# A cap of four on the half-chunk transfers under way in the passes of a Fourier-layer kernel

## The chip, the cores and the metric

The kernel runs on one core of a Trainium2 chip. The metric is the device time of one execution in microseconds (us). Before the change it is 11834.71 us, the median of three runs (11832.55 to 11845.82). All profiles are of one profiled execution.

## The reference, cut to what matters

64 images of 256 x 256 go through four Fourier layers with 32 channels; the result, with 77 text rows appended, goes through one transformer layer. Only the Fourier layers matter here:

```python
v = concat([x, gx, gy]) @ p_w + p_b                  # (64, 32, 256, 256)
for i in range(4):
    x1 = irfft2(mixed low modes of rfft2(v))          # 24 x 12 modes kept
    x2 = einsum('bcxy,cd->bdxy', v, w_w[i]) + w_b[i]
    v  = batchnorm(x1 + x2)                           # mean and variance over b, x, y
    if i < 3: v = relu(v)
out = einsum('bcxy,cu->bxyu', v, q_w) + q_b
...
h = concat([out, txt], axis=1)                        # then attention and a feed-forward with top-k
```

The tensor `v` of one image is 32 x 256 x 256 float32, 8 MB, so that all 64 images do not fit on the chip: `v` goes to device memory after each layer and comes back for the next. The normalisation needs sums over all images, so one layer ends before the next begins.

## The kernel before, in words

The program runs in this order: a first transform of the input and the mixing of modes (to about 200 us of the span); then three **passes**, `layer(0)`, `layer(1)` and `layer(2)`, with mixing of modes between them (`mix`, lines 389 to 486); and a last stage from about 9125 us, which reads `v` once more and runs the transformer (lines 810 to 1147). Pass 0 runs from about 200 to 2749 us, pass 1 from 2884 to 5904, pass 2 from 6041 to 9052.

**A pass** (`layer`, line 531) goes over 64 images of 8 chunks each. A chunk is a tile of 128 partitions x 8 x 256 float32, 1 MB. For a chunk `(b, t)` the function `chunk` (line 732) does this:

- `pre` (line 619): TensorE builds the spectral part from `y_` (line 624: 16 matmul instructions) and, in passes 1 and 2, adds the channel mix of the chunk `vin` loaded from memory (line 635: 32 instructions). ScalarE then writes the first half of the new chunk `vo` through a relu (line 642) and SyncE's queue issues the store of that half, 512 KB (line 643). VectorE writes the second half (line 647; ScalarE at t = 6, line 645) and its store follows (line 648).
- `load_v` (line 585), in passes 1 and 2: the chunk that is needed four chunks later is loaded in two halves of 512 KB (line 589).
- `product` (line 660): the channel mix of the new chunk (line 667: 32 matmul instructions) whose squares ScalarE sums (line 674).
- `turn` (line 650): VectorE transposes the chunk for the coming transform (line 655).

Once per image, at t = 3, TensorE also runs the whole forward transform of the image before (`along_y`, line 685, 256 matmul instructions, and `along_x`, line 712), three products and the `spread` of the next half (line 606). In that stretch few chunks are finished, and few stores issued.

**The order of the work** is written out by hand (the pass is built under `manual_schedule`): each engine runs its instructions in the order of the code. All the transfers of a pass stand in one queue, SyncE's (SP's), in the order store, store, load, load for each chunk; at t = 3 two small loads `ams` (line 573, for the image after the next) and one small store `xh` (line 720) follow. SP is in order: while its head waits, all later transfers wait too.

**What limits the transfers under way before the change.** The completion of SP's transfers is told by eight semaphores, taken in turn. A transfer waits until the one before it on its semaphore has landed, so it waits for the transfer issued eight earlier: at most eight of SP's transfers are under way. Besides, a store needs its half of `vo` written; a load needs a free `vin` buffer (four of them, line 551: the buffer is free when `pre` of four chunks earlier has read it); and a `vo` buffer (four of them, line 553) is written again only when its stores have landed.

In pass 0 there are no chunk loads. Pass 0 loads four small pieces of the image per image instead (`mv`, line 580).

Of the kernel before, what the change touches and what calls it, by code (L numbers as in the profile page):

```python
# [135 lines left out]
def tile_fno_fusion_transformer(ctx: ExitStack, tc: tile.TileContext, a, cst_d, grid_d, out):  # L136
    nc = tc.nc
# [370 lines left out]
    def layer(i, st, src, dst, acc):  # L508
# [7 lines left out]
        with ExitStack() as cx:  # L516
# [47 lines left out]
            y_, t32, vin, vo = {}, {}, {}, {}  # L564

            def two_banks():

                ring[0] += 1
                return pp.tile([128, 2, 512], F32, name=f"ring{ring[0] % 4}")

            def load_am(b):
                for n in range(2):
                    nc.sync.dma_start(
                        ams[b % 2][64 * n:64 * n + 2 * KX],
                        mix_d[i][b].rearrange("p k c -> (p k) c")[:, 512 * n:512 * n + 512],
                    )
# [8 lines left out]
            def load_v(b, t):  # L585
                vin[b, t] = ip.tile([128, 8, S], F32, name="vin")
                for n in range(2):
                    rows = slice(4 * n, 4 * n + 4)
                    nc.sync.dma_start(vin[b, t][:, rows], src[b][:, t, rows])

            def scale_am(b):
                for _, p0, cs in halves:
# [21 lines left out]
            def four():  # L614

                t2 = [two_banks() for _ in range(2)]
                return t2, [t2[n // 2][:, n % 2] for n in range(4)]

            def pre(b, t):
                t2, ps = four()  # L620
                for r in range(2):
                    for n in range(4):
                        q = 8 * (t % 4) + 4 * r
                        nc.tensor.matmul(  # L624
                            ps[n][:, 256 * r:256 * r + 256],
                            lhsT=y_[b, t // 4][32 * n:32 * n + K, q:q + 4, :].rearrange("p q c -> p (q c)"),
                            rhs=mv[b % 2][32 * n:32 * n + K, 2 * t + r, :] if i == 0 else T4[32 * n:32 * n + K, :],
                            start=r == 0, stop=i == 0, skip_group_check=True,
                        )
                if i:  # L630
                    v = vin.pop((b, t))
                    for k in range(4):
                        for n in range(4):
                            j = (n + k) % 4
                            nc.tensor.matmul(  # L635
                                ps[n][32 * j:32 * j + 32], lhsT=ws[32 * n:32 * n + 32],
                                rhs=v[32 * n:32 * n + 32, 2 * j:2 * j + 2, :], start=False, stop=True,
                                skip_group_check=True, tile_position=(32 * n, 32 * j),
                            )
                o = vo[b, t] = op.tile([128, 8, S], F32, name="vo")  # L640
                of = o.rearrange("p (n r) y -> p n (r y)", r=2)
                nc.scalar.activation(of[:, 0:2], t2[0], AF.Relu)  # L642
                nc.sync.dma_start(dst[b][:, t, 0:4], o[:, 0:4])
                if t == 6 or i == 0 and t == 1:
                    nc.scalar.activation(of[:, 2:4], t2[1], AF.Relu)  # L645
                else:
                    nc.vector.tensor_scalar(of[:, 2:4], t2[1], 0.0, None, ALU.max)  # L647
                nc.sync.dma_start(dst[b][:, t, 4:8], o[:, 4:8])

            def turn(b, t):  # L650

# [52 lines left out]
            def along_x(b):  # L704
# [15 lines left out]
                nc.sync.dma_start(xh_d[i][:, b, :], xo.rearrange("p g k -> p (g k)"))  # L720

            load_am(0)
            load_am(1)
            if i == 0:
                load_x(0)
            else:
                for t in range(4):
                    load_v(0, t)
# [3 lines left out]
            def chunk(b, t, done=None):  # L732
                pre(b, t)
                nb, nt = (b, t + 4) if t < 4 else (b + 1, t - 4)
                if i and nb < B:
                    load_v(nb, nt)
                if done is not None:
                    product(*done)
                if t == 5 and b + 1 < B:
                    spread(b + 1, 0)  # L740
                turn(b, t)

            for b in range(B):
                for t in range(8):
                    if b and t == 3:


                        t2, _ = four()
                        along_y(b - 1, t2, range(0, 3))
                        product(b, 0)  # L750
                        along_y(b - 1, t2, range(3, 5))
                        ring[0] -= 2
                        chunk(b, 3)
                        along_y(b - 1, t2, range(5, 8))
                        ring[0] -= 2
                        product(b, 1)
                        product(b, 2)
                    else:
                        last = (b, t - 1) if t else (b - 1, 7)
                        chunk(b, t, None if last[0] < 0 or b and t in (1, 2) else last)  # L760
                    if t == 3:
                        spread(b, 1)
                        if b + 2 < B:
                            load_am(b + 2)
                        if b:
                            along_x(b - 1)
                    if i == 0 and t == 0 and b + 1 < B:
                        load_x(b + 1)
                    if t == 7 and b + 2 < B:
                        scale_am(b + 2)  # L770
# [6 lines left out]
    for i in range(L):  # L777
# [26 lines left out]
        if i < L - 1:  # L804
            acc = const.tile([128, 16 * B], F32, name="acc") if acc is None else acc
            with tc.manual_schedule():
                layer(i, st, vd[(i + 1) % 2], vd[i % 2], acc)


    src = vd[L % 2]  # L810
# [87 lines left out]
    rows = [128, 128, TXT]  # L898
# [283 lines left out]
```

## Time and profile before

| what | value |
|---|---|
| median of 3 runs | 11834.71 us |
| the profiled execution's own time | 11830.89 us |
| its span, first to last instruction | 11829.1 us |
| mean granted TensorE clock | 0.976 |
| TensorE (PE) busy | 10902.5 us, 92% |
| VectorE (DVE) busy | 8539.0 us, 72% |
| ScalarE (ACT) busy | 6507.0 us, 55% |
| HBM read and written | 1761.87 MB and 1696.92 MB |
| stores `v<-vo` | 3072 of 512 KB |
| loads `vin<-v` | 2048 of 512 KB |

The page gives the busy time of each engine, then the span cut into 40 equal slices (295.7 us each) with the busy share of each engine in tenths, the busy share of the 16 DMA engines and the rate in GB/s. Passes 1 and 2 are slices 10 to 31 or so. A wait is shown with what released it; "issue" means that the engine waited for nothing that the profile can name. The queue q1 carries SP's transfers, q8 carries the engines' instruction blocks. Beside the page the trace holds each packet of each DMA queue (start, duration, bytes) and each increment of the semaphores that tell of a landing; a transfer of 512 KB is 128 packets of 4096 bytes, eight on each of the 16 DMA engines, and its landing is 16 increments, one from each DMA engine.

### The profile page before, as it was taken

Reading aid. Unit: us, or ns where it says so; the run is one execution under the profiler, and the core shown is the slowest. Engines: PE = TensorE matmul, PEld = TensorE weight load, DVE = VectorE, ACT = ScalarE, POOL = GpSimd, SP = SyncE. Lnnn points to the kernel's source line nnn. Section 1 sums busy time; section 2 is a strip of 40 time slices with the busy share of each in tenths; the row PEclk is TensorE's granted clock in tenths of the full one; section 3 lists DMA queues with packets and bytes.
Section 4 is the critical chain, followed back from the end, with each engine's and each line's share of the span. In section 5 each row is a group of like instructions: output and inputs, shape, how many; then the busy total and the mean of one; then the engine's idle time right before and its main releaser. Section 6 shows DMA issues by size and latency. Waiting matters only on the chain. (4 is left out here: it accounts for less than half of the span.)

```text
span 11829.1 us, 409923 instructions
## 1 busy us (share of the span) xinstructions
PE 10902.5 (92%) x182038; PEld 5901.9 (50%) x182038; DVE 8539.0 (72%) x10405; ACT 6507.0 (55%) x10697; POOL 1327.2 (11%) x1987
## 2 busy tenths in 40 slices
PE   6999999996999999999969999999997899999999
PEld 3444444443444444444434444444444566666666
DVE  6888888886777777777767777777776666666665
ACT  5766767665555555555555555555555333333333
POOL 0000000001000000000010000000001233333333
PEclk8999999998999999999979999999998899999999
DMA  7666666667999999999989999999998656555553
GB/s 231 226 227 223 230 223 227 226 223 266 360 367 368 359 361 361 366 359 360 358 311 366 370 361 360 364 366 365 357 361 305 259 215 235 224 222 236 215 230 144
DMA packets 957962, 3485.55 MB, mean 295 GB/s; under 512 B 135960, under 2 KB 185496, under 8 KB 884888
## 3 DMA queue, kind: packets, MB, share of 16 engines
q1 hardware_dynamic: 908160, 3393.01, 75.0%
q0 software_dynamic: 40880, 62.59, 2.1%
q8 instruction: 1424, 23.33, 0.8%
q10 hardware_dynamic: 7144, 3.72, 0.1%
q14 instruction: 354, 2.90, 0.1%
HBM read 1761.87 MB, written 1696.92 MB: 292 GB/s over the span
## 5 line engine op out<-in xcount | busy, mean ns | idle before, releaser
L655 DVE STREAM_TRANSPOSE t<-vo 128x2048 f32<-128x2048 f32 x1536 | 3535.8, 2305 | 214.3 <-ACT vo L645 97.4
L674 ACT ACTIVATE ring<-ring 128x1024 f32<-128x1024 f32 x3072 | 3112.7, 1013 | 1031.4 <-PE ring L667 980.7
L667 PE MATMUL ring<-vo,w 32*32 32x512 f32 x49152 | 2611.2, 599 | 245.4 <-DVE zt L699 153.1
L647 DVE TENSOR_SCALAR vo<-ring 128x1024 f32<-128x1024 f32 x1280 | 1553.0, 1213 | 1533.5 <-PE ring L635 956.7
L642 ACT ACTIVATE vo<-ring 128x1024 f32<-128x1024 f32 x1536 | 1571.1, 1023 | 1492.5 <-PE ring L635 1270.1
L685 PE MATMUL ring<-t,cst 32*32 32x512 f32 x49152 | 2212.3, 599 | 123.7 <-issue 123.0
L667 PEld LDWEIGHTS ring<-vo,w 32*32 32x32 f32 x49152 | 826.6, 103 | 1356.6 <-issue 571.5
L685 PEld LDWEIGHTS ring<-t,cst 32*32 32x32 f32 x49152 | 978.6, 103 | 995.9 <-issue 681.0
L624 PE MATMUL ring<-cst,y 24*128 24x256 f32 x16384 | 1388.7, 404 | 50.4 <-ACT vo L645 27.0
L624 PEld LDWEIGHTS ring<-cst,y 24*128 24x128 f32 x16384 | 896.2, 184 | 918.5 <-ACT vo L642 460.9
L594 POOL TENSOR_TENSOR ams<-ams,bns 48x512 f32<-48x512 f32 x384 | 400.9, 1044 | 8124.4 <-DMA ams<-mix 6615.5
L635 PE MATMUL ring<-vin,ws 32*32 32x512 f32 x32768 | 1279.9, 604 | 13.6 <-issue 7.9
L610 DVE STREAM_TRANSPOSE y<-ring 128x1024 f32<-128x1024 f32 x384 | 755.7, 1968 | 331.7 <-PE ring L606 331.7
L624 PE MATMUL ring<-mv,y 29*128 29x256 f32 x8192 | 736.0, 407 | 43.5 <-ACT ring L674 20.5
L624 PEld LDWEIGHTS ring<-mv,y 29*128 29x128 f32 x8192 | 459.4, 185 | 469.7 <-ACT vo L642 168.4
L712 PEld LDWEIGHTS ring<-cst,zt 128*128 128x128 f32 x4608 | 533.6, 193 | 154.4 <-issue 108.9
L674 ACT ACTIVATION_READ_ACCUMULATOR ring<-ring 128x1 f32 x3072 | 585.0, 190 | 0.0
L1131 POOL DMA_DIRECT2D out_dram<-o x1024 | 505.0, 502 | 659.2 <-DVE o L1126 629.5
L712 PE MATMUL ring<-cst,zt 128*128 128x96 f32 x4608 | 565.6, 280 | 8.2 <-DVE zt L699 8.2
L697 ACT COPY half<-ring 128x1024 f32<-128x1024 f32 x192 | 194.4, 1012 | 574.9 <-PE ring L685 574.9
L635 PEld LDWEIGHTS ring<-vin,ws 32*32 32x32 f32 x32768 | 263.4, 103 | 434.7 <-issue 365.2
L930 PE MATMUL hp<-ch,win 128*32 128x512 f32 x4096 | 473.0, 602 | 6.5 <-DMA ch<-v 6.4
(367 smaller groups left out, 9981.9 us busy)
## 6 DMA issues: line engine op xcount, KB each, us to landing
v<-vo SPq DMA_DIRECT2D x3072, 512.0 KB
vin<-v SPq DMA_DIRECT2D x2048, 512.0 KB
ch<-v SPq DMA_DIRECT2D x512, 1024.0 KB
mix<-ob SPq DMA_DIRECT2D x96, 512.0 KB
ams<-mix SPq DMA_DIRECT2D x384, 96.0 KB
xin<-in_x_dram SPq DMA_DIRECT2D x16, 1024.0 KB
mv<-in_x_dram SPq DMA_DIRECT2D x256, 64.0 KB
out_dram<-o POOLq DMA_DIRECT2D x1024, 16.0 KB, 3.0
```

The source lines that it names most:

```text
L610: nc.vector.transpose(y_[b, h].rearrange("p q c -> p c q"), ps.rearrange("p n (c k) -> p (n c) k", k=32))
L624: nc.tensor.matmul(ps[n][:, 256 * r:256 * r + 256], lhsT=y_[b, t // 4][32 * n:32 * n + K, q:q + 4, :].rearrange("p q c -> p (q c)"), rhs=m ...
L635: nc.tensor.matmul(ps[n][32 * j:32 * j + 32], lhsT=ws[32 * n:32 * n + 32], rhs=v[32 * n:32 * n + 32, 2 * j:2 * j + 2, :], start=False, sto ...
L642: nc.scalar.activation(of[:, 0:2], t2[0], AF.Relu)
L647: nc.vector.tensor_scalar(of[:, 2:4], t2[1], 0.0, None, ALU.max)
L655: nc.vector.transpose(t32[b, t // 2][:, :, 8 * (t % 2):8 * (t % 2) + 8, :].rearrange("p y s c -> p s y c"), o.rearrange("p s (y l) -> p s ...
L667: nc.tensor.matmul(ps[n][32 * j:32 * j + 32], lhsT=w4[i + 1][32 * n:32 * n + 32], rhs=o[32 * n:32 * n + 32, 2 * j:2 * j + 2, :], start=Tru ...
L674: nc.scalar.activation(t2[n], t2[n], AF.Square, accum_out=acc[:, at:at + 1])
L685: nc.tensor.matmul(ps[n][32 * j:32 * j + 32], lhsT=FYT[32 * n:32 * n + 32, k, :], rhs=t32[b, j][32 * n:32 * n + 32, k].rearrange("p s c -> ...
L712: nc.tensor.matmul(ps[:, 0, 96 * g:96 * g + 96], lhsT=zt[:, h, k0:k0 + 4, :].rearrange("p k c -> p (k c)"), rhs=FX[:, h, 48 * r:48 * r + 9 ...
L930: nc.tensor.matmul(hp[32 * g:32 * g + 32], lhsT=win[:, 7 - t:39 - t], rhs=ch[:, g], start=False, stop=t == 7, skip_group_check=True,)
L1131: nc.gpsimd.dma_start(out[b, 64 * n + 16 * g:64 * n + 16 * g + 16].rearrange("(p t) d -> p t d", t=2), o[32 * g + 8 * n:32 * g + 8 * n + 8 ...
```

## The change

Each of the half-chunk transfers of a pass (the loads of line 589, the stores of lines 643 and 648) is issued through a helper `move`, which keeps a list of them and adds a dependency of each on the completion of the fourth one before it. `moves` is a list of the pass: it starts empty in each of the three passes. The transfers `ams`, `mv` and `xh` are neither in the list nor do they wait on it.

```diff
+            moves = []
+
+            def move(to, of):
+
+                moves.append(nc.sync.dma_start(to, of).ins)
+                if len(moves) > 4:
+                    tc.add_manual_dep(
+                        moves[-1], moves[-5].name,
+                        mybir.DependencyInfo(mybir.DependencyClass.Sync, mybir.DependencyReason.DATA),
+                        reason="four chunk transfers at a time",
+                    )
+
...
-                    nc.sync.dma_start(vin[b, t][:, rows], src[b][:, t, rows])
+                    move(vin[b, t][:, rows], src[b][:, t, rows])
...
-                nc.sync.dma_start(dst[b][:, t, 0:4], o[:, 0:4])
+                move(dst[b][:, t, 0:4], o[:, 0:4])
...
-                nc.sync.dma_start(dst[b][:, t, 4:8], o[:, 4:8])
+                move(dst[b][:, t, 4:8], o[:, 4:8])
```

The instructions of TensorE, VectorE, ScalarE and GpSimd are the same, in the same order; SP issues the same transfers in the same order, with other waits.

## The prediction

> **What bounds the kernel now.** First the page's slices, for where the DMA engines are full.
>
> ```profile
> span 11829.1 us, 409923 instructions
> PE   6999999996999999999969999999997899999999
> DMA  7666666667999999999989999999998656555553
> GB/s 231 226 227 223 230 223 227 226 223 266 360 367 368 359 361 361 366 359 360 358 311 366 370 361 360 364 366 365 357 361 305 259 215 235 224 222 236 215 230 144
> q8 instruction: 1424, 23.33, 0.8%
> ```
>
> Pass 0 (slices 2 to 9) has a full TensorE and DMA engines at six tenths. In passes 1 and 2 (slices 11 to 31) both are full. They last 3019.8 us and 3011.6 us from first store to last (SP's issues in the timeline), 6031 us together for 128 images: 47.1 us per image. Only there does the cap bind. q8 brings instructions.
>
> Then a single image in 1.5 us stretches (columns after the two times: PE, PEld, DVE, ACT, POOL busy, clock, DMA share, GB/s).
>
> ```profile
> 3519.50:3521.00 1.50, 1.50 (x48) 0.74 (x41) 0.00 (x0) 0.04 (x1) 0.00 (x0) 1.00 0.67 234
> 3521.00:3522.50 1.50, 1.50 (x48) 0.50 (x31) 0.92 (x1) 0.97 (x1) 0.00 (x0) 1.00 0.20 64
> 3527.00:3528.50 1.50, 1.50 (x20) 0.83 (x16) 0.98 (x1) 1.48 (x4) 0.00 (x0) 1.00 0.97 235
> 3548.00:3549.50 1.50, 1.50 (x59) 1.03 (x60) 1.27 (x1) 0.27 (x1) 0.00 (x0) 1.00 1.02 418
> 3551.00:3552.50 1.50, 0.23 (x12) 0.00 (x0) 0.00 (x0) 0.37 (x2) 0.00 (x0) 1.00 0.99 396
> ```
>
> The DMA engines run at some 415 GB/s, but fall dry for about 3 us once an image (the stretch at t = 3, in which no stores come), and then run at 235 to 300 GB/s for 5 us. And at 3551, in the full-rate part, TensorE, VectorE and ScalarE all stand still. Why, the waits tell; first pass 1 (3100 to 5700 us), then pass 0 (800 to 2500 us).
>
> ```profile
> SPq L589 <- DMA vin<-v: 384.3, 472, 2.4
> PEld ring L667 <- issue: 228.5, 627, 2.6
> PEld ring L685 <- issue: 222.8, 454, 2.7
> DVE vo L647 <- DMA v<-vo: 77.7, 18, 6.8
> PEld ring L635 <- DMA vin<-v: 23.6, 45, 1.7
> ```
>
> ```profile
> PEld ring L685 <- issue: 110.5, 390, 0.4
> PEld ring L667 <- issue: 28.2, 85, 0.3
> ```
>
> TensorE hardly waits for loaded data (23.6 us), nor VectorE for a free `vo` (77.7). It waits for nothing nameable, up to 2.7 us at a time, where pass 0 has 0.4 at most. The timeline at such a place:
>
> ```profile
> 3549.39 1.84 PE L685 MATMUL ring<-t,cst 32*32 32x512 f32 x45
> 3551.71 1.55 SPq L589 DMA_DIRECT2D vin<-v  x2
> 3552.99 1.05 PE L685 MATMUL ring<-t,cst 32*32 32x512 f32 x5 [1.76 <-issue]
> ```
>
> No semaphore is waited for. The trace has one q8 packet here, 16,384 bytes, from 3550.56 to 3551.56; TensorE goes on 1.4 us after its end. That delay is 1.40 us on average in the 308 stalls of this kind (no semaphore, over 0.4 us, just after a q8 packet) in 2884-5840 and 6030-8990 us. They sum to 355 us. So in passes 1 and 2 **TensorE starves for instructions**. I counted them by the chunk transfers in flight when the q8 packet starts (issue to last landing):
>
> ```
> in flight      0-3   4    5    6    7    8
> q8 packets     145  53   57   78  131  439
> with a stall     0   0    1   10   41  256
> us to next q8    -  5.0  5.3  5.9 6.0  6.0   (medians, pass 1)
> ```
>
> With eight in flight a block comes every 6.0 us, nearly whatever the code (tenth to seventy-fifth percentile 5.9 to 6.1): supply sets that pace. In pass 0 intervals go down to 3.2 us.
>
> **What the Trainium skill says.** The Trainium skill's page Runtime: NRT & Kernel Launch, "Instruction fetch mechanics": instructions are refilled in 16 KiB blocks of 256 through a DMA queue of the sequencer's own, mostly hidden. The packet size agrees; hidden it is not, with 355 us of stalls. Its page DMA: Bandwidth & Descriptors, "Queues, rings and completion order": each DMA engine serves its queues in turn, a packet of about 9 to 17 descriptors at a time. By that an instruction block waits for one such packet, whatever lies behind it, and the depth would not matter; the table speaks against it, though fetch rate and depth may both follow the stage of the image. [...] Here a lone store (1500.96 us) lands 2.63 us after its issue, of which 8 x 159 ns = 1.27 us is data: 1.36 us fixed.
>
> **The change part by part.**
>
> (1) *The waits.* 5120 transfers (1024 in pass 0, 2048 in each other) wait on the fourth last instead of the eighth last. Behind a waiting SP stand its next stores, loads, `ams` and `xh`; their users are `pre` four chunks on, a `vo` four chunks on, and the next image but one. SP's order is kept and the DMA queue is first in, first out, so as long as it never runs dry each transfer lands as before, just issued later. Does it? At full rate one transfer lands each 1.26 us, so four in flight mean 5.0 us from issue to landing, above the 2.63 us of a lone one. The slowest DMA engine always has work: 0. In pass 0 two stores come per chunk, and the fourth last is two chunks old; only behind the `mv` loads (landings 10 to 11 us after issue) is SP held, by 0.9 and 1.7 us in the image at 1517 us, and `vo` has four chunks of slack: 0. If that cover fails, it is the slower rival.
>
> (2) *The instruction blocks.* At four in flight the interval is 5.0 us in place of 6.0 (table). So each of the 308 stalls shrinks by up to 1.0 us; taken stall by stall 99 us of 355 remain. Removed: 256 us, times 6031/5916 for the whole passes: 261 us. Bounds: 0, if depth is not the cause; 362 us, if all goes.
>
> (3) *What is late next.* The DMA engines. Their packets in the two passes: 2 x 2593 us at 159 ns, 310 us excess of slow packets, 140 us small transfers, 59 us q8, 4 us q14; so they idle 334 of 6031 us (2.6 us per image). If TensorE gains 261 us, that idle shrinks to 73 us, 0.6 us per image, and `vo` and `vin` waits (77.7 + 23.6 + some 81 on other landings in 2600 us) grow. I let a tenth of the gain be lost there, my choice between none and a third: 261 x 0.9 = 235 us. The bursts of slow packets follow the dry spells; if the dry spell closes they go too, up to 310 us. I count none of this.
>
> Sum: 11830.9 - 235 = 11596 us for the profiled execution, which lies 3.8 us below the median; so **11600 us**.
>
> **Rivals.**
>
> *No change.* Instruction blocks wait for one packet of whatever queue is non-empty, as the arbitration on that page has it; the table's correlation is that of the stage (TensorE's bursts fall where eight are in flight). For it: between a stall's end and the next block's start lie 3.7 us whatever the depth then. Against it: pass 0 runs the same bursts (lines 685, 667) and never waits over 0.4 us, and of 255 packets at up to five in flight one stalled. Or the gain is made and lost at once on `vo`. 11,820 to 11,850.
>
> *Small gain.* Lagging DMA engines still hold four transfers of backlog when a block comes, so half the stalls' shrinkage fails: 50 to 120 us, 11,715 to 11,785.
>
> *Slower: the leading DMA engines run dry and fall into step.* The 16 shares of one transfer land spread: that of 3549.27 us has its first after 7.07 us and its last after 9.90, a lead of 2.8 us. At four in flight, when the last share lands three transfers are queued (3.8 us), and a new one needs 1.3 us to come: a leader over 2.5 us ahead stands still. Those that stand restart together, and the switches between stores and loads in step are what costs in the 5 us after each dry spell (the first two stores after 3522 us have all shares within 0.4 us of each other, and the next landings lie 1.8 to 2.4 us apart instead of 1.26). The excess there is 310/128 = 2.4 us over some 8 transfers, 0.3 us each. If it spreads to 16 more of an image's 32 transfers: 16 x 0.3 x 128 = 614 us, less the 235: 12,210. It decides from about 6 transfers per image (6 x 0.3 x 128 = 230 us). Against it: each leader need only lose 0.3 us once to be back within 2.5, and 15 of the 16 shares that land about 3536 lie within 1.3 us. Likeliest size 11,900 to 12,200.
>
> *More than forecast.* All stalls go (362 us), and slow packets with the dry spells: 11,300 to 11,470.
>
> **How the numbers follow.** Forecast (11,470 to 11,715) 0.50; more 0.07; small gain 0.11; no change 0.13; slower 0.19. The range reaches from 11,440 to 11,850, which leaves out the slower case and the far end of the greater gain. About 0.2% (24 us) is what a measurement can tell from no change: faster 0.68, same 0.13, slower 0.19. As cases of both signs hold weight, the likeliest one's own range is 11,470 to 11,715.
>
> **What would show it.** Right: in pass 1 PEld waits on "issue" at lines 667 and 685 fall to about a third with longest near 1.5 us; blocks come at 5 us and less; SP waits on transfers far more; passes of 45.2 us per image; DMA rate in slices 11 to 30 up from 363 to some 378 GB/s; pass 0 unchanged. Wrong: stalls as long as before at four in flight (no change); or slow packets well beyond the 5 us after a dry spell, with the excess above 310 us (slower). A longer pass 0 would refute part 1.

## The result and the profile after

The changed kernel takes **11883.3 us** (median of six runs, 11875.0 to 11893.7), beside 11840.3 us of the kernel before on the same chips (six runs; the 11834.7 us given above are the median of three of them): a ratio of 1.0037, 95% interval 1.0024 to 1.0050. It is slower by 0.4%. The forecast was 11600 us, faster.

The page after, with its DMA queue line, shows the two kernels side by side.

```profile
span 11877.7 us, 409612 instructions
DMA  7666666668999999999999999999998655656553
...
GB/s 231 227 227 225 227 223 230 221 227 265 363 364 363 364 359 359 359 366 363 340 313 358 361 357 359 363 359 359 364 356 302 261 225 221 236 214 235 222 227 145
...
q1 hardware_dynamic: 908160, 3393.01, 77.0%
```

Pass 0 and the last stage are as they were. In passes 1 and 2 the DMA engines are *busier* than before (q1 holds 77.0% of 16 engines' span, 75.0% before, and its bytes are the same) and yet move no more per second: 356 to 366 GB/s in most slices, 357 to 370 before. The mean time of a packet has grown. The same image place as in the prediction, in 1.5 us stretches (last two columns: DMA share and GB/s; before them the granted clock, and after the two times PE, PEld, DVE, ACT and POOL):

```profile
3519.50:3521.00 1.50, 1.50 (x56) 0.72 (x61) 0.00 (x0) 0.04 (x1) 0.00 (x0) 1.00 1.01 407
3524.00:3525.50 1.50, 1.50 (x60) 0.50 (x31) 1.45 (x2) 1.05 (x3) 0.00 (x0) 1.00 0.83 301
3536.00:3537.50 1.50, 1.50 (x51) 0.82 (x64) 1.45 (x2) 1.06 (x3) 0.00 (x0) 1.00 0.91 295
3542.00:3543.50 1.50, 0.06 (x4) 0.00 (x0) 1.39 (x2) 0.13 (x1) 0.00 (x0) 1.00 0.89 336
3548.00:3549.50 1.50, 1.50 (x48) 0.72 (x31) 1.39 (x2) 0.40 (x1) 0.00 (x0) 0.50 0.92 344
```

The dry spell at t = 3 is gone (the first line had 0.67 and 234 GB/s, the next 64). In its place the rate drops to some 300 GB/s every few microseconds, all through the image, where before it stayed near 415. And at 3542 TensorE stands still again. The waits of pass 1 (3100 to 5700 us; line 679 was 667, 697 was 685, 647 was 635) say for what:

```profile
PEld ring L679 <- issue: 180.6, 587, 1.9
PEld ring L697 <- issue: 165.0, 413, 2.4
PEld ring L647 <- DMA vin<-v: 142.4, 171, 3.0
```

The waits for nothing nameable fell (228.5 and 222.8 before). The wait of line 647 for its loaded chunk rose from 23.6 to 142.4 us: that is the **new wait**. In the same 2600 us the first two fell by 106 us together, and the third rose by 119 us. (Line 647's own waits on "issue" fell as well, from 159.1 to 105.7 us.) The timeline at 3541 shows such a wait:

```profile
3541.14 1.55 SPq L575 DMA_DIRECT2D v<-vo  x2
3544.67 0.14 PEld L647 LDWEIGHTS ring<-vin,ws 32*32 32x32 f32 x4 [3.01 <-DMA vin<-v]
3544.67 1.05 PE L647 MATMUL ring<-vin,ws 32*32 32x512 f32 x4 [2.61 <-DMA vin<-v]
```

Loads stand four chunks ahead in SP's order, and still some land too late. From the issues and landings of pass 1: the first load of a chunk is issued a median 12.9 us before TensorE begins to use the chunk (19.1 us before the change), since SP holds it back, and the second half lands a median 5.2 us ahead of that moment (7.7 us before); for a tenth of the chunks it lands 1.0 us or more after it. SP shows the cap at work, with two lines of its own waits in the same window, and below them the two of the stores before the change:

```profile
SPq L575 <- DMA vin<-v: 943.4, 851, 3.3
SPq L575 <- DMA v<-vo: 824.4, 786, 3.0
```

```profile
SPq L643 <- DMA v<-vo: 232.2, 253, 1.9
SPq L648 <- DMA v<-vo: 146.8, 178, 2.1
```

1768 of 2600 us are waits for landings; before they were 763 (these two lines and the 384.3 us of line 589 in the prediction).

**The balance.** From the packet records of the trace: passes 1 and 2 together, from first store to last, in us. "Slow packets" is what the 4096-byte packets took beyond 159 ns each, divided by 16 engines; "idle" is the passes' time less all packets' time; "stalls" are TensorE's instruction stalls, counted as in the prediction over the whole passes.

```
kernel                          passes 1+2   slow packets   idle   stalls
before (eight under way)          6031.4        310.1      333.5    361.2
the change (four)                 6079.8        578.7      110.1    145.0
```

Slow packets +268.6, idle -223.4: +45.2 of the +48.4 us. This is an account whose parts make up the passes' time by construction: it says where the time lies, not what put it there. The median packet takes 159 ns as before. In pass 1 the packets of over 250 ns went from 3.3% to 4.85% of those of 4096 bytes, and they hold most of the excess (83% before, 91% after). The stalls fell nearly as forecast, and the passes became no shorter.

One more thing got worse. In passes 1 and 2 TensorE's granted clock stood at 0.50 in 42 stretches, most of them 3.4 us long, where before there were 9. By the clock records that is 87 us of full-clock time lost, against 17. The extra 70 us are more than the 48 us that the passes lost, and no run separates this from the slower transfers. It goes with the waits for loads: with five under way (below) the load wait of pass 1 is 46.4 us, and 15 us of clock are lost.

### The profile page after: what moved, and what is told of

Same layout as the page of the kernel before. It is cut to its first block, busy times and chain, and to the rows that moved or that the text cites. A ratio compares the mean times of both kernels' runs of the same rounds, so it can differ in the third digit from the quotient of the medians.

```text
span 11877.7 us, 409612 instructions
## 1 busy us (share of the span) xinstructions
PE 10919.7 (92%) x182038; PEld 5967.7 (50%) x182038; DVE 8544.3 (72%) x10405; ACT 6511.0 (55%) x10697; POOL 1332.7 (11%) x1987
## 5 line engine op out<-in xcount | busy, mean ns | idle before, releaser
L679 PE MATMUL ring<-vo,w 32*32 32x512 f32 x49152 | 2581.7, 599 | 235.8 <-DVE zt L711 194.8
L697 PE MATMUL ring<-t,cst 32*32 32x512 f32 x49152 | 2241.1, 610 | 50.9 <-issue 50.2
L647 PE MATMUL ring<-vin,ws 32*32 32x512 f32 x32768 | 1349.6, 615 | 145.5 <-DMA vin<-v 144.5
L697 PEld LDWEIGHTS ring<-t,cst 32*32 32x32 f32 x49152 | 1022.9, 104 | 876.9 <-issue 562.3
```

The costliest lines, as they stand in the source:

```text
L647: nc.tensor.matmul(ps[n][32 * j:32 * j + 32], lhsT=ws[32 * n:32 * n + 32], rhs=v[32 * n:32 * n + 32, 2 * j:2 * j + 2, :], start=False, sto ...
L679: nc.tensor.matmul(ps[n][32 * j:32 * j + 32], lhsT=w4[i + 1][32 * n:32 * n + 32], rhs=o[32 * n:32 * n + 32, 2 * j:2 * j + 2, :], start=Tru ...
L697: nc.tensor.matmul(ps[n][32 * j:32 * j + 32], lhsT=FYT[32 * n:32 * n + 32, k, :], rhs=t32[b, j][32 * n:32 * n + 32, k].rearrange("p s c -> ...
```

## The experiments

Two theories stood at the start. **A (depth):** four transfers do not keep the DMA engines at full rate when stores and loads mix, whatever else runs. **B (the held queue):** SP's waits make stores and loads late, and computation makes the transfers slow. C to G are named where they arise.

### Transfers alone

The passes are replaced by the transfers, with no computation:

```diff
+        stages = [
+            ("SS", 8), ("SS", 4), ("LL", 8), ("LL", 4),
+            ("SSLL", 8), ("SSLL", 6), ("SSLL", 5), ("SSLL", 4), ("SSLL", 3),
+            ("SLSL", 4), ("SSSSLLLL", 4), ("SSSSLLLL", 8),
+        ]
...
+                for f, b, t, n in todo:
+                    f(b + 8 * (k % 7) if f is store else b, t, n, 1 if first else depth)
```

> All computation is left out (the outputs are zeros): after 128 stores that fill the source, twelve stages of transfers of 512 KB alone, each begun after the one before it has landed. SS is stores alone and LL loads alone (128 transfers each), SSLL the order of the passes, SLSL and SSSSLLLL other orders (256 each); the number is how many are under way. Theory A (depth): switches between stores and loads cost the DMA engines time when only four transfers are queued, with or without computation. Then SS and LL take 1.26 us per transfer at 8 and at 4, SSLL at 8 takes 1.26 to 1.30, SSLL at 4 1.40 to 1.50, at 6 and 5 between, and SSSSLLLL at 4 has half the switches and about half the loss. Theory B (the held queue): the loss comes from the computation, through loads and stores that SP issues late; then SSLL at 4 takes 1.26 to 1.30 like SSLL at 8.

The stages SS at 4, LL at 4, then SSLL at 8, 6, 5, 4 and 3, SLSL at 4 and SSSSLLLL at 4 (time, then the last two columns, DMA share and GB/s):

```profile
337.20:504.00 166.80, 0.00 (x0) 0.00 (x0) 1.00 1.01 402
671.80:838.60 166.80, 0.00 (x0) 0.00 (x0) 1.00 1.01 402
838.60:1165.20 326.60, 0.00 (x0) 0.00 (x0) 1.00 1.01 411
1165.30:1492.50 327.20, 0.00 (x0) 0.00 (x0) 1.00 1.02 410
1492.50:1827.60 335.10, 0.00 (x0) 0.00 (x0) 1.00 1.01 401
1827.70:2175.30 347.60, 0.00 (x0) 0.00 (x0) 1.00 1.01 386
2175.30:2592.40 417.10, 0.00 (x0) 0.00 (x0) 1.00 0.92 322
2592.40:2920.90 328.50, 0.00 (x0) 0.00 (x0) 1.00 1.02 409
2920.90:3266.80 345.90, 0.00 (x0) 0.00 (x0) 1.00 1.01 388
```

Per transfer (length over 256): SSLL 1.276 us at eight, 1.278 at six, 1.309 at five, 1.358 at four, 1.629 at three. Stores or loads alone lose nothing at four. So A holds in kind and B is not needed: four under way cost 0.08 us per transfer with no computation. The sizes were missed: A had 1.40 to 1.50 us at four, and a loss at six. Nor is it a price per switch from stores to loads, as I had guessed: SSSSLLLL has half the switches and loses nearly as much (1.351 us, and 1.282 at eight), SLSL has the most and loses next to nothing (1.283). Each stage is one measurement. SSLL at four came out at 1.358, 1.361, 1.384 and 1.373 us in the four kernels of transfers alone on this page, so a difference of 0.03 us between two kernels says little.

### Six in place of four

```diff
-                if len(moves) > 4:
-                        moves[-1], moves[-5].name,
+                if len(moves) > 6:
+                        moves[-1], moves[-7].name,
```

> The change with six transfers in place of four. In the trace of before, blocks of instructions that came at six in flight stalled TensorE for 0.12 us on average, against 0.7 at eight. Theory A: most of the stall goes (355 us to under 150), while the excess of slow packets stays nearer to the 310 us of before than to the 579 us of four; 11,720 to 11,820 us. Theory B: a held queue costs in proportion to the cap; 11,850 to 11,870 us. A third case, that six keeps the stalls of eight: 11,830 to 11,850 us.

11820.1 us, ratio 0.9987 (0.9979 to 0.9995). Slow packets 325.1 us as A had it, but the stalls stayed: 347.1 us. It is the third case but for its time, which lies just under it, at the upper edge of A's range. The 0.12 us that I had read off the trace of before at six in flight misled. A possible reason, not tested: those transfers were counted when the block's packet began, some 3.7 us after the stall before had ended, so that the queue may have been deeper when the wait began.

### Stores alone wait, loads alone wait

```diff
-            def move(to, of):
+            def move(to, of, held):
...
-                if len(moves) > 4:
+                if held and len(moves) > 4:
```

with `held` true for the stores and false for the loads, and the reverse.

> Only stores wait on the fourth last transfer; loads are issued right behind them (up to six in flight). Theory A, with the loss at the switch from stores to loads because too few loads are queued: the loads are queued earlier, the excess of slow packets falls well below 579 us, 11,760 to 11,830 us. Theory B: the stores are held as in the change, their vo buffers come free late, 11,870 to 11,890 us.

> Only loads wait on the fourth last transfer; stores do not (up to six in flight). Theory A: loads are still queued late, the excess stays at 500 us or more, 11,850 to 11,890 us. Theory B: loads have four chunks of slack and stores are no longer held, 11,780 to 11,840 us.

Stores only: 11856.9 us, ratio 1.0024 (1.0017 to 1.0031), slow packets 604.0, stalls 160.3. Loads only: 12055.0 us, ratio 1.0187 (1.0173 to 1.0201), slow packets 669.1, stalls 287.2. Neither came out as expected. Loads queued early did not recover the rate (604.0 against 578.7), which speaks once more against "too few loads behind the stores". That loads-only costs 1.9% fits neither theory as I had put it; why it is so much worse than the full cap stays open.

### The alternate order: at four, at eight, at three

Store, load, store, load for each chunk; only the place of the loads in SP's queue changes:

```diff
                 move(dst[b][:, t, 0:4], o[:, 0:4])
+                load_next(b, t, 0)
...
                 move(dst[b][:, t, 4:8], o[:, 4:8])
+                load_next(b, t, 1)
...
-                if i and nb < B:
-                    load_v(nb, nt)
```

> The change with another order in SP's queue: store, load, store, load for each chunk, the same transfers and the same cap of four. With transfers alone this order took 1.283 us per transfer at four under way, against 1.358 in the order of the passes. Theory A, that the change loses by that rate what it gains in instruction supply: the stalls stay low (about 145 us in passes 1 and 2), the excess of slow packets falls from 579 us to 250 to 400 us, and the time is 11,600 to 11,750 us. Theory B, that the computation makes the transfers slow (or that the dry spells come back in another place): 11,840 to 11,890 us.

> The same order, but the eighth last in place of the fourth last, so that only the order of before is changed. Theory A: the order alone frees no instruction supply (stalls 340 to 370 us) and at eight the order of the passes already runs at full rate: within 20 us of before, 11,815 to 11,855 us. Theory B': the order, and not the cap, is what helps; then it is as fast as the run at four, under 11,750 us.

> The same order with three under way. Theory A: the last stalls go (under 60 us in passes 1 and 2); if three transfers (3.8 us at full rate, 2.6 us for a lone one) still keep the DMA engines full, 11,550 to 11,720 us; if they run dry as the order of the passes did at three (1.63 us per transfer), over 12,200 us.

At four: 11831.5 us, ratio 1.0002 (0.9994 to 1.0010), stalls 119.8 but slow packets 594.1. The prediction from transfers alone failed: in the kernel the alternate order at four loses the rate too. At eight: 11745.9 us, ratio 0.9929 (0.9917 to 0.9942). I had expected no change; slow packets fell from 310.1 to 231.1, which is most of the 86 us that the passes gained. The time is what theory B' had asked for, but not for its reason, since the same order at four is no faster than the kernel before. At three: 12596.8 us, ratio 1.0652 (1.0636 to 1.0669), stalls only 50.1, slow packets 901.7 and idle 491.5: the branch "they run dry".

### Transfers alone again

```diff
+            ("SLSL", 8), ("SLSL", 5), ("SLSL", 4), ("SLSL", 3), ("SLSL", 2),
+            ("SSLL", 7), ("SSLL", 4), ("SSLL", 8), ("SLL", 4),
```

> All computation is left out again (the outputs are zeros); stages of transfers alone: SLSL at 8, 5, 4, 3, 2, then SSLL at 7, 4, 8, then store, load, load (SLL, 192 transfers) at 4. Expected per transfer: SLSL 1.27 to 1.29 down to 4; at 3 1.28 to 1.40; at 2 at least 1.32 (half of 2.63), likelier 1.5; SSLL as before at 4 (1.36) and 8 (1.28), at 7 1.28. If runs of two of one kind are the cause, SLL at 4 lies between 1.28 and 1.36; if alternation in step with the cap is, SLL is as bad as SSLL or worse.

SLSL: 1.264 us at eight and five, 1.266 at four, then 1.577 at three and 1.771 at two, far above what I had expected there (1.28 to 1.40, and some 1.5). SSLL at four 1.361 as in the first run, at seven 1.280. SLL at four 1.368: as bad as SSLL. So alone the alternate order is safe down to four; something in the kernel takes that away.

### Other packets among them

Theory C, that the instruction blocks do: a transfer of 16 KB on GpSimd's queue after each fifth.

```diff
+            ins = nc.gpsimd.dma_start(t, flat_grid[4096 * (k % 64):4096 * (k % 64) + 4096].rearrange("(o y) -> o y", o=1)).ins
+            tc.add_manual_dep(
+                ins, moves[-4].name,
...
```

> All computation is left out once more (zeros come out); stages of 256 transfers alone, some with a transfer of 16 KB in one piece on GpSimd's queue after each fifth (about each 6.3 us, as the instruction blocks come in the passes). Stages: SLSL at 8; SLSL at 8, 6 and 5 with blocks; SLSL at 4 without and with; SSLL at 8 without and with; SSLL at 4 without and with. A block costs 1 us of one DMA engine in 16, about 0.01 us per transfer where nothing else suffers. Theory C, that blocks set back one DMA engine at a time, so that the others run out of queued transfers at a small cap: SLSL at 4 goes from 1.27 to 1.33 or more with blocks, SLSL at 8 stays at 1.27 to 1.29. Rival D, that the computation (late stores, small transfers, its memory traffic) is what spoils the alternate order at four: blocks leave SLSL at 4 at 1.27 to 1.29.

SLSL at 8 without and with blocks, at 5 with, at 4 without and with:

```profile
170.10:493.90 323.80, 0.00 (x0) 0.00 (x0) 1.00 1.02 415
494.00:821.00 327.00, 0.00 (x0) 24.35 (x50) 1.00 1.02 413
1148.20:1476.40 328.20, 0.00 (x0) 24.22 (x50) 1.00 1.02 412
1476.40:1805.50 329.10, 0.00 (x0) 0.00 (x0) 1.00 1.02 408
1805.60:2154.00 348.40, 0.00 (x0) 24.22 (x50) 1.00 1.01 388
```

At four, blocks take the rate from 1.286 to 1.361 us per transfer; at eight from 1.265 to 1.277, about their own time (0.01 us, the estimate above), and at five with blocks it is 1.282. In the order of the passes they cost 0.027 us at eight (1.277 to 1.304) and 0.039 at four (1.384 to 1.423). For the alternate order at four that is what C forecast and not what D did. It does not show that the computation and the small transfers add nothing in the kernel. One difference from the kernel: these blocks went as 16 packets of 1024 bytes, not as one of 16,384, so it shows that strange packets suffice to spoil four, not that a setback of one DMA engine by 1.2 us is needed.

### Five and six

> Alternate order with five under way (four gave 11,831 us, eight 11,746 us). Theory C: one more transfer covers one block (1.2 us of setback), so the excess of slow packets falls near that of eight (230 us in passes 1 and 2) while part of the stalls goes; 11,680 to 11,750 us. Rival D, a loss in proportion to the cap: about 11,800 us.

> Alternate order with six. In the order of the passes six kept the stalls of eight (347 against 361 us) and the excess too. Expected the same here: 11,720 to 11,750 us, stalls 300 to 330 us.

> The change with five in place of four, in the order of the passes. Transfers alone lost 0.03 us each at five, 0.08 at four, none at six. Theory A: an excess of slow packets of 380 to 480 us, stalls of 200 to 300 us, 11,800 to 11,850 us; anything above the change's time would speak against a price that shrinks with depth.

The number in `move` alone is edited: five and six in the alternate order, and five in the order of the passes. The change with **five** in place of four: 11706.4 us, ratio 0.9891 (0.9877 to 0.9904). In the alternate order five gives 11629.7 us, **0.9827** (0.9814 to 0.9840), the fastest kernel here, and six 11738.5 us, 0.9919 (0.9906 to 0.9933), as expected. Both kernels with five are faster than expected: slow packets and stalls of the one in the order of the passes came out in their ranges, but its idle time fell too, from 333.5 to 116.5 us, which I had not counted. The stretch 4000 to 5000 us in pass 1 of the change, of five, and of five in the alternate order:

```profile
4000.00:5000.00 1000.00, 938.26 (x19415) 474.98 (x19407) 723.08 (x398) 572.41 (x898) 43.94 (x42) 0.98 0.98 359
```

```profile
4000.00:5000.00 1000.00, 957.53 (x19870) 484.47 (x19884) 740.58 (x408) 589.34 (x928) 45.94 (x44) 1.00 0.98 368
```

```profile
4000.00:5000.00 1000.00, 958.32 (x20331) 490.00 (x20330) 753.73 (x416) 598.07 (x939) 45.96 (x44) 1.00 0.97 375
```

At nearly the same DMA share, the rate goes from 359 to 368 to 375 GB/s, and TensorE's instructions in the stretch from 19415 to 20331. The whole series, as in the balance above. Each row is one profiled execution; that of alternate, four was 23 us slower than the median of its runs, the others lay within 17 us of theirs:

```
order, under way       passes 1+2   slow packets   idle   stalls
passes, eight            6031.4        310.1      333.5    361.2
passes, six              6027.3        325.1      313.8    347.1
passes, five             5921.9        416.0      116.5    212.9
passes, four             6079.8        578.7      110.1    145.0
alternate, eight         5945.4        231.1      333.0    325.8
alternate, six           5940.1        229.0      330.1    323.9
alternate, five          5827.5        260.2      186.5    214.6
alternate, four          6054.3        594.1       69.2    119.8
alternate, three         6788.7        901.7      491.5     50.1
```

Stalls fall with every transfer taken away from six down; slow packets rise steeply from five to four. In both orders five is the best that was measured. A slower kernel asks for its instructions more slowly, and would stall less for that alone; but with five the kernels are faster and stall less. The quickest blocks also come sooner with fewer under way: in pass 1, in the order of the passes, a tenth of the blocks began within 5.5 us of the block before at eight and at six, within 5.0 us at five, and within 4.65 us at four.

### The same bytes in other pieces

What makes four too few? E: the lead that it leaves to the faster DMA engines; F: the bytes under way; G: the number of transfers.

```diff
+        stages = [
+            (2, 8), (2, 4), (4, 8), (4, 7), (4, 6), (1, 4), (1, 3), (1, 2),
+        ]
...
+            w = 8 // parts
+            move(dst[b][:, t, w * n:w * n + w], vo[t % 4][:, w * n:w * n + w], depth)
```

> All computation is left out (zeros come out); 64 chunks per stage, stores of a chunk and then its loads, with the chunk cut in two (512 KB), in four (256 KB) or not at all (1 MB). Stages: 512 KB at 8 and 4; 256 KB at 8, 7 and 6; 1 MB at 4, 3 and 2. Per 512 KB moved. Theory E, that what counts is the lead which the cap leaves the faster DMA engines, all queued transfers but the one that is landing, less 1.3 us: 512 KB at 4 leaves 2.5 us, 256 KB at 8 leaves 3.1, at 7 2.5, at 6 1.9; 1 MB at 4 leaves 6.3, at 3 3.7, at 2 1.2. Then 256 KB at 8 loses less than 512 KB at 4 (1.30 to 1.34), at 7 as much (1.36), at 6 more (1.40 to 1.50); 1 MB at 3 loses nearly nothing (1.28 to 1.31) and at 2 most (1.5 or more). Rival F, that the bytes under way count: 256 KB at 8 and 1 MB at 2 are like 512 KB at 4, 1.36. Rival G, that the number of transfers counts: 256 KB at 8 1.28, 1 MB at 4 1.36, at 3 1.6.

512 KB at 8 and 4; 256 KB at 8, 7 and 6; 1 MB at 3 and 2:

```profile
170.00:497.50 327.50, 0.00 (x0) 0.00 (x0) 1.00 1.01 410
497.60:849.10 351.50, 0.00 (x0) 0.00 (x0) 1.00 1.00 382
849.10:1194.10 345.00, 0.00 (x0) 0.00 (x0) 1.00 1.04 389
1194.10:1557.40 363.30, 0.00 (x0) 0.00 (x0) 1.00 1.02 370
1557.40:1947.00 389.60, 0.00 (x0) 0.00 (x0) 1.00 0.99 345
...
2265.30:2583.30 318.00, 0.00 (x0) 0.00 (x0) 1.00 1.01 422
2583.40:2940.60 357.20, 1.76 (x1) 0.00 (x0) 1.00 0.97 378
```

Packets of 2048, 4096 and 8192 bytes take 84, 159 and 309 ns (medians), so 512 KB cost 1.344, 1.272 and 1.236 us at best. Beyond that: 256 KB at eight 0.004 us, at seven 0.075, at six 0.18; 512 KB at four 0.10; 1 MB at three 0.006, at two 0.16. With the same 2 MB under way the loss is 0.004, 0.10 or 0.16 us by the size of the pieces, which excludes F; eight of 256 KB are safe, but so are three of 1 MB, which excludes G. In the order of E's lead (3.7 us and more: 0.01; 3.1: 0.004; 2.5: 0.075 and 0.10; 1.9: 0.18; 1.2: 0.16) it rises nearly in step. E fits best of the three, but its sizes were off too: it put 1 MB at two worst of all, at 1.5 us or more, where it took 1.395, less beyond its best than 256 KB at six. My numbers had also left out that smaller packets are dearer and larger ones cheaper.

## Why the prediction was wrong, point by point

- **What bounds the kernel: right.** TensorE's instruction supply in passes 1 and 2 does depend on the transfers under way. Stalls fell at four (361 to 145), at five (213, in a faster kernel), at three in the alternate order (50). (Its "pass 0 has 0.4 at most" holds for lines 667 and 685; lines 606, 624 and 712 wait up to 0.8 us there. And three line numbers ahead of the prediction are off: `layer` begins at 508, the buffers of `vin` are set at 520 and those of `vo` at 521 to 524.)
- **Step 1, "the slowest DMA engine always has work: 0": wrong, and this is the step that failed.** The DMA queue stayed filled in the sense that I checked (5.0 us against a lone transfer's 2.6), but the rate did not: transfers alone lost 0.08 us each at four, an estimated 330 us for the 4096 of the two passes. In the kernel slow packets rose by 269 us, where the prediction had 0. For pass 0 the zero was right (2547.8 us before and after), though SP was held more than it said: 299 us for landed stores in 1700 us, up to 6.7 us at a time.
- **Step 2, 261 us of stalls removed: right in kind, somewhat large.** 216 us went, and 145 us remained where 99 had been reckoned.
- **Step 3: half right.** The DMA engines' idle time shrank as forecast (to 110 us; 73 forecast). But I held the slow packets at 310 us, and expected them to go with the dry spells if anything. They nearly doubled.
- **The rival "slower: the leading DMA engines run dry"** had the threshold right: a lead of more than 2.5 us is cut off at four. The landings of the trace of before show a lead of 1.5, 2.7 and 3.4 us (tenth, fiftieth and ninetieth percentile of passes 1 and 2), so over half of the transfers were beyond it. I set it aside with "each leader need only lose 0.3 us once", which no view showed. By the same arithmetic five leaves 3.7 us, above the ninetieth percentile, and six 5.0. The runs agree only roughly: six adds almost nothing to the slow packets (325), but five adds 106 us, in which leads beyond 3.7 us (3.5% of the transfers) can hardly have a large part. The 269 us of four are 7 transfers of each image at its 0.3 us, by its own arithmetic, where its sum had 16; so 11883 lies just under its likeliest range. That the leaders "fall into step" was not shown.
- **"No change" and "small gain"** are out: the supply did improve, and the gain was made and lost on the DMA engines, not on `vo` (line 659 waited 80.4 us for it in pass 1, 77.7 before).
- **What would show it:** the issue waits fell by a quarter, not to a third; the DMA rate did not rise (359 GB/s from 4000 to 5000 us, 362 before); slow packets are all through the image. That is the sign named for the slower case.

That four under way are enough to slow the transfers is thus shown by the transfers alone, and that this cap takes the gain, by the runs with five. The balance and the load waits say where the gain went: into packets that take longer, and into TensorE's waits for loads that they delay. How much of it is due to the lower clock is open. *Why* a DMA engine that has been cut off costs slow packets rather than idle time (switching in step was my word for it) was not settled; the alternate order alone has leads of only 0.8 to 1.1 us, close to step, and no loss.

## What to carry to other kernels

A cap on transfers under way has two sides, a queue shallow enough for instruction blocks to pass and deep enough for the spread between DMA engines. Measure that spread from the landings (first to last share), and start from the smallest cap whose lead, (n - 1) transfers less the reissue time, covers its ninetieth percentile: here 3.4 us in the order of the passes and 2.8 in the alternate order at eight, which gives five for both. It is a place to start and no more. The alternate order alone with blocks spread by 1.8 us at eight (ninetieth percentile), and four, which leave 2.5, still lost. A lone transfer's round trip is no measure of it. When a gain rests on a cap, try the numbers on both sides: one transfer more made this change 1.1% faster than before instead of 0.4% slower.

## What the runs showed of the hardware that was not expected

- With eight transfers of 512 KB under way, half of the instruction blocks (16,384 bytes) of pass 1 came 6.0 to 6.5 us after the block before; at six this had hardly changed (5.9 to 6.5).
- Between the first and the last of the 16 shares of a transfer lay 2.7 us in the median in the kernel before, 2.2 us in the alternate order at eight, and 0.8 us with that order at eight alone.
- The order of stores and loads in one queue matters at full depth: alternating them took the slow packets from 310 to 231 us, and 0.7% off the kernel.
- After TensorE had stood still for 2.6 us on a load, its granted clock was 0.50 in the stretch at 3548 us (table above). In passes 1 and 2 of the slowest variant (three under way) there were 142 stretches at 0.50, against 9 before; its mean clock was 0.941, against 0.976.
- Pieces of 1 MB (8192 bytes per packet) move at 422 GB/s with three under way; 512 KB move at 410 with eight.
